# Transposing the first element's attended rows: TensorE into PSUM, or VectorE in 32x32 blocks and DRAM

## The chip, the cores and the metric

The kernel runs on one core of a Trainium2 chip. The metric is device time in microseconds (us) of one execution. The kernel before takes 826.79 us, the median of 3 runs (826.36 to 827.36).

A core has TensorE (PE: matmuls, with a separate weight load, PEld), VectorE (DVE), ScalarE (ACT), GpSimd (POOL) and SyncE (SP). Here SP issues nearly all DMA transfers. Each engine runs its own list of instructions in order and waits on semaphores of the others.

## The reference, cut to what matters

There are 4 elements of 512 tokens with 512 features. A cross-attention with 32 heads of 16 features is added to x, then an FFN is added.

```python
x = x + _L0_xattn_ref(_layernorm(x, axis=-1), ctx_1024, pos, pos, Wq, Wkv, Wout, bout)
x = x + _L0_ffn_ref(_layernorm(x, axis=-1), w_fc, w_proj)

# inside the FFN
h = bitlinear(x, w_fc)                    # layer norm, rounding that all but cancels, ternary weights
h = jax.nn.gelu(h, approximate=False)
return bitlinear(h, w_proj)
```

The FFN's first product is over the features. TensorE contracts over partitions, and x lies with tokens on the partitions. So the normalized rows after attention, called d here, must be turned: features on the partitions, tokens along the row. They are also split into a rounded high part and a low remainder[...].

## The kernel before, in words

**Attention.** The 4 elements have 8 groups of 4 heads each: 32 groups, counted from 0. A group works on 8 tiles (units) of each of three kinds, each tile 128 x 1024:

- Logits `lp` (`logits`, L526): TensorE multiplies queries and keys. VectorE takes the row maxima `mx` (`maxima`, L540).
- Scores `sp` (`exponentials`, L565 and L573): TensorE computes the transposed logits and subtracts the maxima by a second matmul. ScalarE takes the exponential `es` (L577).
- Products `av` (`weigh`, L587): TensorE multiplies exponentials and values, after each second unit.

The tiles `lp` and `sp` share one pool of three buffers, `ps_s`, each a pair of PSUM banks. A new tile takes one that an earlier tile has left: logits are left by VectorE, scores by ScalarE.

The order of the instructions on all five engines is written out by the program itself, which records them in the order in which Python calls them. A list of bursts holds three tiles each, scores and logits mixed. The logits run 12 to 15 units ahead of the scores. Between the bursts a planner puts small jobs (class `Chore`: projections, transposes) as a running credit allows. `put_off(k, f, 1)` defers a call to the end of burst k. The maxima of a whole group are turned by TensorE (`mtp`, L552), copied by ScalarE (`mrows`) and used by all its scores.

**The last element.** Groups 24 to 31 belong to the last element. During them, the first element's x is complete, and its FFN input is prepared, in four token tiles of 128 rows:

- `stats` (L730): VectorE computes mean and variance (`st`, `mv`), GpSimd the inverse deviation `r_a`. It is called in group 29, units 0 to 3.
- `prepare` (L739): VectorE writes the normalized rows `d`. It is called in group 30, units 0, 2, 4 and 6.
- `first_chore` and `first_T` (L780, L797): TensorE transposes the four 128x128 blocks of `d` into the PSUM buffer `tp_d` (L788). VectorE casts it to the high part `dTh` (L792) and subtracts for the low part `dTl` (L793). The jobs stand at the end of the planner's queue and run in group 31.

After the last group, the first matmuls of the FFN (`first`, `hp`, L1083) read `dTh` and `dTl` of element 0.

**The other elements** take another way, inside the FFN of the element before: `prepare`, then `turn` (L746: VectorE transposes in 32x32 blocks, `turned`), then `place` (L753: four DMAs lay the blocks in DRAM so that the whole is transposed), then `fetch_T` (L762: one DMA brings the tile back into `dTl`), then `split_T` (L772: ScalarE casts to `dTh`, VectorE subtracts in place).

SP also carries the stores and loads of the attended rows (`av_d`, `den`, `rden_d`, `rb`) and the loads of the FFN's second weights (`wproj`, two after each of the last four groups).

The functions that the change touches:

Of the kernel before, what the change touches and what calls it, by code (L numbers as in the profile page):

```python
# [9 lines left out]
F32 = mybir.dt.float32  # L10
F32R = mybir.dt.float32r
AF = mybir.ActivationFunctionType
ALU = mybir.AluOpType
# [18 lines left out]
def xattn_ffn(  # L32
# [264 lines left out]
    def put_off(k, f, end=0):  # L297
        later[end].setdefault(k, []).append(f)
# [440 lines left out]
    def prepare(i, pool, tag, bufs=2):  # L739
        d = pool.tile([P, D], F32, name=f"d{i}", tag=tag, bufs=bufs)  # L740
        nc.vector.tensor_scalar(
            d, x_sb[:, i, :], mv1[i][:, 0:1], f1[i], ALU.subtract, ALU.mult
        )
        return d

    def turn(i, d, pool, tag, bufs):  # L746

        b, t = divmod(i, NT)
        turned = pool.tile([P, D // HP, HP], F32, name=f"turned{i}", tag=tag, bufs=bufs)
        nc.vector.transpose(turned.rearrange("p n j -> p (n j)"), d)  # L750
        return turned

    def place(i, turned):  # L753
        b, t = divmod(i, NT)
        to = turned_d[b].rearrange("(n i) s -> i n s", i=HP)
        for a in range(P // HP):
            nc.sync.dma_start(
                to[:, :, t * P + a * HP : t * P + (a + 1) * HP],
                turned[a * HP : (a + 1) * HP],
            )  # L760
# [8 lines left out]
            turned_d[b].rearrange("(k p) s -> p k s", p=P)[:, :, cols],  # L769
        )  # L770

    def split_T(i):  # L772
        b, t = divmod(i, NT)
        if t == 0:
            dT[b][0] = big.tile([P, KD, S], F32R, name=f"dTh{b}", tag="aT", bufs=2)
        high, low = (x[:, :, t * P : (t + 1) * P] for x in dT[b])
        nc.scalar.copy(high, low.bitcast(F32))
        nc.vector.tensor_tensor(low, low.bitcast(F32), high.bitcast(F32), ALU.subtract)

    def first_T(i, d, tp, e):  # L780
        b, t = divmod(i, NT)
        if t == 0:
            dT[b] = (
                big.tile([P, KD, S], F32R, name=f"dTh{b}", tag="aT", bufs=2),
                big.tile([P, KD, S], F32R, name=f"dTl{b}", tag=f"va{b % 2}"),
            )
        for k in range(KD):
            nc.tensor.transpose(tp[:, k, :], d[:, k * P : (k + 1) * P], ident)  # L788

        def split():  # L790
            high, low = (x[:, :, t * P : (t + 1) * P] for x in dT[b])
            e(high, tp)  # L792
            nc.vector.tensor_tensor(low, tp, high.bitcast(F32), ALU.subtract)  # L793

        return split

    def first_chore(t, ready):  # L797
        split = []

        def step(p, _):  # L800
            tp = p.rearrange("p (k n) -> p k n", k=KD)
            split.append(first_T(t, first_d.pop(t), tp, nc.vector.tensor_copy))

        return Chore(f"tp_d{t}", 1, step, lambda p, k: put_off(k + 1, split[0]), 0.7, ready)


    n_groups = B * NG
# [96 lines left out]
    def when(i, u=0):  # L904
        return burst_of["s", i * NU + u]
# [17 lines left out]
    queue += a + projections(1) + c2 + c3  # L923
    n_prep = len(queue)
    queue += projections(2)
    queue += [first_chore(t, when(n_groups - 2, 2 * t + 1) + 1) for t in range(NT)]
    n_queue = len(queue)
    loads_behind = {
        f"kpk{b}_3": lambda b=b: (load_ctx(b + 1), load_trig(b + 1)) for b in range(B - 1)
# [7 lines left out]
    wanted = []  # L937
    urgent = []
    due = []
    av, es, first_d = {}, {}, {}  # L940
    open_chore = None
    credit = 0.0

    for k, burst in enumerate(bursts):
        run(k)
        for kind, s in burst:
            i, u = divmod(s, NU)
            if kind == "l":
                lp = logits(i, u)
                maxima(i, u, lp)  # L950
                if u == NU - 1:
                    urgent.append((k + 1, place_maxima(i)))
                continue
            b, g = divmod(i, NG)

            if u == 6 and 4 <= i + 3 < n_groups:
                wanted.append(i + 3)
            while wanted and {(wanted[0] // NG, wanted[0] % NG // 2, w) for w in "kq"} <= stored:
                load_stacks(wanted.pop(0))
            if (i, u) in loads_at:  # L960
                loads_at[i, u]()
            if u % 2 == 0 and (b == 0 and g == 0 or b < 2 and g == 5):
                norm1(b + 1 + (g > 0), u // 2)
            if u % 2 == 0 and u // 2 < XH and (b == 0 and g == 1 or b < 2 and g == 7):
                normed(b + 1 + (g > 1), u // 2)
            if g == 5 and u % 2 == 0:
                add_bias(b, u // 2)
            if u in (2, 6):
                c = 2 * i + u // 4
                if c < 2 * NW:  # L970
                    sum_chunk(c, k)
                c -= 18
                if 0 <= c < 2 * NW:
                    sign_chunk(c, k)
            if u == 6 and i in (8, 16):
                urgent.append((k, mean_abs(i // 8 - 1, (gam_fc, gam_pr)[i // 8 - 1])))
            if b == B - 1:
                if g >= NG - NS and u == NU - 1:
                    load_second(i)
                if g == 4 and u == 0:  # L980


                    wfc_sb = []
                    for n, tag in enumerate(("w0", "w1", "w4", "w5")):
                        wfc_sb.append(big.tile([P, F], F32R, name=f"wfc{n}", tag=tag))
                        nc.sync.dma_start(wfc_sb[n].bitcast(F32), wfc_d[n * P : (n + 1) * P, :])
                if g == 5 and u < NT:
                    stats(u)
                if g == 6 and u % 2 == 0:
                    first_d[u // 2] = prepare(u // 2, apool, "xh", XH)  # L990
            es[u] = exponentials(i, u)
            if u % 2:
                due.append((k + 1, i, u // 2, (es[u - 1], es[u])))
        run(k, 1)

        while due and due[0][0] <= k:
            _, j, c, e = due.pop(0)
            if c == 0:
                av[j] = ps_v.tile([P, S], F32, name=f"av{j}", tag="v")
            weigh(j, c, e, av[j])  # L1000
            if c == NT - 1:
                put_off(k + 1, lambda j=j, k=k: attended(j, av.pop(j), k + 1))

        credit = min(credit + (RATE if n_queue - len(queue) < n_prep else RATE_END), 3.0)
        used_bank = False
        next_urgent = urgent[0][0] if urgent else 10**6

        g_next = min(
            (burst_of["l", j * NU + NU - 1] + 1
             for j in range(n_groups)  # L1010
             if ("l", j * NU + NU - 1) in burst_of and burst_of["l", j * NU + NU - 1] + 1 >= k),
            default=10**6,
        )
        next_urgent = min(next_urgent, g_next)
        while True:
            if open_chore is None:
                if urgent and urgent[0][0] <= k:
                    if used_bank:
                        break
                    open_chore = urgent.pop(0)[1]  # L1020
                    open_chore.urgent = True
                elif queue and queue[0].ready <= k and not used_bank and credit >= queue[0].cost:
                    c = queue[0]
                    if next_urgent <= k or c.steps > 2.2 * (next_urgent - k):
                        break
                    open_chore = queue.pop(0)
                    open_chore.urgent = False
                else:
                    break
            left = open_chore.steps - open_chore.done  # L1030
            must = open_chore.urgent or next_urgent - k <= 1
            if not must and credit < open_chore.cost:
                break
            credit -= open_chore.cost
            if open_chore.go():
                if open_chore.name in loads_behind:
                    put_off(k + 1, loads_behind[open_chore.name], 1)
                open_chore.post(open_chore.p, k)
                open_chore = None
                used_bank = True  # L1040
# [138 lines left out]
    with tc.manual_schedule(engines=ordered):  # L1179
# [14 lines left out]
        for n in range(len(steps) + 4):  # L1194
# [21 lines left out]
            if on and b + 1 < B:  # L1216
                at = (10, 11, 12, 13) if b == 0 else (8, 10, 12, 13)
                for t in range(NT):
                    i = (b + 1) * NT + t
                    if f == at[t] - 6:  # L1220
                        stats(i)
                    elif f == at[t] - 4:
                        d = prepare(i, fpool, "d", 1)
                        place(i, turn(i, d, fpool, "turned", 1))
                        fetch_T(i)
                    elif f == at[t]:
                        split_T(i)
            if n == 3:
                nc.vector.tensor_copy(ones_r, ones)
            if n == 7:  # L1230
# [86 lines left out]
```

## Time and profile before

| What | us |
| --- | --- |
| Median of the runs | 826.79 |
| Profiled execution, its own time | 826.86 |
| Its span | 825.1 |
| PE busy | 803.9 |
| DVE busy | 609.7 |
| ACT busy | 472.3 |
| POOL busy | 300.2 |
| Transposes of d on TensorE (L788), start of the first and last | 551.5, 562.7 |
| Statistics of element 0 (L733), first to last start | 524.3, 533.6 |
| First FFN matmul (L1083) | 564.1 |
| Block transposes (L750), 12, mean | 0.712 |

A line of the profile names the source line, engine, operation, and the output and input tiles (`out<-in`). "Idle before" with an arrow names what ended an idle time. The chain is followed back from the last instruction of the execution, at each step to what released it. Times in a timeline count from the start of the span.

### The profile page before, as it was taken

What the parts mean: (1) busy time and instruction counts of PE and PEld (TensorE: products, weight loads), DVE (VectorE), ACT (ScalarE), POOL (GpSimd) and SP (SyncE); (2) the same over time, 40 slices, a digit from 0 to 9 for tenths busy, and PEclk for the clock granted to TensorE, in tenths of its full rate; (3) what the DMA queues carried; (4) which work ended last, traced back from release to release, by engine and by line L of the source; (5) the groups of instructions that cost most, each with busy time, mean ns of one, the idle gap of its engine ahead of it and who ended that gap; (6) DMA issues with size and microseconds to landing.
All of it is one profiled execution on the core that took longest, in us unless ns stands there. A gap on an engine that the chain in (4) does not pass through costs nothing.

```text
span 825.1 us, 14410 instructions
## 1 busy us (share of the span) xinstructions
PE 803.9 (97%) x5524; PEld 424.0 (51%) x5524; DVE 609.7 (74%) x846; ACT 472.3 (57%) x664; POOL 300.2 (36%) x299
## 2 busy tenths in 40 slices
PE   9999999999999999999999999999999999999996
PEld 5234443344343334433343334336668888888884
DVE  7798677787868888778767876855746885875755
ACT  3257667676675556656555665576335455555542
POOL 2546275563933656576515731210200210211001
PEclk9999999999999999999999999999999999999999
DMA  7768596578785477968644677443130140240101
GB/s 252 217 211 299 189 317 220 176 245 282 238 288 194 169 283 232 314 197 274 215 154 165 224 228 276 149 140 105 40 63 14 40 101 14 68 87 0 52 1 51
DMA packets 107604, 139.94 MB, mean 170 GB/s; under 512 B 37776, under 2 KB 45456, under 8 KB 107024
## 3 DMA queue, kind: packets, MB, share of 16 engines
q1 hardware_dynamic: 106608, 138.38, 51.2%
q8 instruction: 43, 0.70, 0.4%
q10 hardware_dynamic: 928, 0.66, 0.3%
q14 instruction: 25, 0.20, 0.1%
HBM read 80.87 MB, written 57.08 MB: 167 GB/s over the span
## 4 chain that ended last, share of the span: by engine, by line
PE 79%; DVE 11%; DMA 4%; issue 2%; ACT 1%; POOL 1%; SPq 1%; ACTq 0%; DVEq 0%; POOLq 0%
PE hp L1083 14%; PE fp L1121 14%; PE av L587 12%; PE sp L565 7%; PE lp L526 7%; DVE mx L540 6%; PE sp L573 5%; PE op L346 4%; PE qpq L346 4%; PE kpk L346 3%; PE vp L346 3%; PE op L1207 2%; DMA q_st<-q_d 2%; PE mtp L552 2%; DVE ws L684 1%
## 5 line engine op out<-in xcount | busy, mean ns | idle before, releaser
L540 DVE TENSOR_REDUCE mx<-lp 128x2 f32<-128x1024 f32 x256 | 305.1, 1216 | 98.6 <-PE lp L526 98.3
L577 ACT ACTIVATE es<-sp 128x1024 f32<-128x1024 f32 x256 | 254.5, 1025 | 138.7 <-PE sp L573 129.0
L587 PE MATMUL av<-es,va 128*32 128x512 f32 x1024 | 136.2, 604 | 0.0
L565 PE MATMUL sp<-q_st,k_st 64*128 64x512 f32 x512 | 114.5, 443 | 6.3 <-DVE mx L540 5.5
L526 PE MATMUL lp<-k_st,q_st 64*128 64x512 f32 x512 | 112.3, 435 | 3.9 <-DMA q_st<-sl_q 1.9
L1091 ACT ACTIVATE h<-hp,gam_fc 128x512 f32<-128x512 f32 x64 | 44.1, 689 | 116.8 <-PE hp L1083 114.5
L573 PE MATMUL sp<-mrows,sel 64*128 64x512 f32 x512 | 101.4, 392 | 0.2 <-ACT mrows L556 0.2
L1121 PE MATMUL fp<-wproj,hh 128*128 128x512 f32 x256 | 101.0, 394 | 0.0
L1083 PE MATMUL hp<-dTh,wfc 128*128 128x512 f32 x256 | 100.2, 392 | 0.0
L1083 PE MATMUL hp<-dTl,wfc 128*128 128x512 f32 x256 | 99.8, 390 | 0.0
L1121 PE MATMUL fp<-wproj,hl 128*128 128x512 f32 x256 | 99.7, 389 | 0.0
L565 PEld LDWEIGHTS sp<-q_st,k_st 64*128 64x128 f32 x512 | 48.0, 184 | 79.4 <-DVE mx L540 37.9
L526 PEld LDWEIGHTS lp<-k_st,q_st 64*128 64x128 f32 x512 | 48.2, 185 | 75.4 <-ACT es L577 41.9
L1110 DVE TENSOR_TENSOR acc<-acc,h 128x512 f32<-128x512 f32 x56 | 39.5, 706 | 54.8 <-ACT h L1091 54.8
L626 POOL TENSOR_TENSOR aT<-aT,rb 128x512 f32<-128x512 f32 x16 | 21.3, 1333 | 130.1 <-DMA rb<-rden_d 126.9
L346 PE MATMUL qpq<-xT,wq_sb 128*32 128x512 f32 x512 | 62.9, 594 | 0.7 <-ACT xT L383 0.7
L1157 POOL TENSOR_TENSOR m<-m 128x4 f32<-128x4 f32 x4 | 0.8, 201 | 158.6 <-DVE m L1156 158.6
L1083 PEld LDWEIGHTS hp<-dTh,wfc 128*128 128x128 f32 x256 | 48.0, 188 | 11.6 <-DVE dTh L792 0.8
L1121 PEld LDWEIGHTS fp<-wproj,hh 128*128 128x128 f32 x256 | 48.1, 188 | 10.8 <-issue 0.9
L1121 PEld LDWEIGHTS fp<-wproj,hl 128*128 128x128 f32 x256 | 48.1, 188 | 10.7 <-issue 0.7
L1083 PEld LDWEIGHTS hp<-dTl,wfc 128*128 128x128 f32 x256 | 48.1, 188 | 10.0
L573 PEld LDWEIGHTS sp<-mrows,sel 64*128 64x128 f32 x512 | 48.3, 185 | 6.0 <-ACT mrows L556 0.8
(154 smaller groups left out, 1054.8 us busy)
## 6 DMA issues: line engine op xcount, KB each, us to landing
k_st<-k_d SPq DMA_DIRECT2D x31, 512.0 KB
q_st<-q_d SPq DMA_DIRECT2D x31, 512.0 KB
av_d<-avs SPq DMA_DIRECT2D x32, 256.0 KB
k_d<-sh_k SPq DMA_DIRECT2D x30, 256.0 KB
k_d<-sl_k SPq DMA_DIRECT2D x30, 256.0 KB
q_d<-sh_q SPq DMA_DIRECT2D x30, 256.0 KB
q_d<-sl_q SPq DMA_DIRECT2D x30, 256.0 KB
wm<-in_wfcT SPq DMA_DIRECT2D x16, 256.0 KB
```

What stands on the lines that cost most here:

```text
L346: nc.tensor.matmul(p[j * HP : (j + 1) * HP, :], w[:, j * HP : (j + 1) * HP], x, start=start, stop=stop,)
L526: nc.tensor.matmul(lp[:, h, :], q_st[i][rows, r, t * P : (t + 1) * P], k_st[i][rows, r, :], start=True, stop=True,)
L540: nc.vector.tensor_reduce(mx[i][:, t, :, r], lp, AX.X, ALU.max, negate=True)
L565: nc.tensor.matmul(sp[:, h, :], k_st[i][rows, r, c * P : (c + 1) * P], q_st[i][rows, r, :], start=True, stop=False,)
L573: nc.tensor.matmul(sp[:, h, :], sel[rows, r, :], mrows[i][rows, :], start=False, stop=True)
L577: nc.scalar.activation(es, sp, AF.Exp, scale=1.0 / math.sqrt(HD))
L587: nc.tensor.matmul(av[j * HP : (j + 1) * HP, :], va[b % 2][:, c, v0 : v0 + HP], es[r][:, h, :], start=c == 0, stop=c == NT - 1,)
L626: nc.gpsimd.tensor_tensor(aT[b][:, n, :], aT[b][:, n, :], rb, ALU.mult)
L1083: nc.tensor.matmul(hp, wfc_sb[k][:, f * P : (f + 1) * P], dT[b][half][:, k, :], start=half == 0 and k == 0, stop=half == 1 and k == KD - 1,)
L1091: nc.scalar.activation(hid[b, f], hp, AF.Gelu, scale=gam_fc[:, 0:1])
L1110: nc.vector.tensor_tensor(acc[b][0], old, x, ALU.add)
L1121: nc.tensor.matmul(outs[b][t], parts[b, f][half][:, t * P : (t + 1) * P], wproj_sb[f], start=half == 0 and f == 0, stop=half == 1 and f == ...
```

## The change

Element 0 now takes the way of the other elements, inside the attention of the last element:

- The statistics are called in group 28, units 0 to 3, one group earlier.
- In group 29, units 0, 2, 4 and 6, `prepare` is followed at once by `turn`. Both tiles come from the pool tag `xh` with three buffers.
- `place` is deferred by one burst, `fetch_T` by four.
- In group 31, units 0, 2, 4 and 6, GpSimd casts the high part; one burst later VectorE subtracts for the low part.
- The four planner jobs with 16 TensorE transposes are gone, and with them the casts and subtractions that read PSUM.
- `split_T` is divided into `high_T` and `low_T`. The other elements use ScalarE for the first as before.

```diff
+    def high_T(i, e):
         b, t = divmod(i, NT)
         if t == 0:
             dT[b][0] = big.tile([P, KD, S], F32R, name=f"dTh{b}", tag="aT", bufs=2)
-        high, low = (x[:, :, t * P : (t + 1) * P] for x in dT[b])
-        nc.scalar.copy(high, low.bitcast(F32))
+        high, low = parts_T(i)
+        e(high, low.bitcast(F32))
+
+    def low_T(i):
+        high, low = parts_T(i)
         nc.vector.tensor_tensor(low, low.bitcast(F32), high.bitcast(F32), ALU.subtract)
...
-    queue += [first_chore(t, when(n_groups - 2, 2 * t + 1) + 1) for t in range(NT)]
...
-                if g == 5 and u < NT:
+                if g == 4 and u < NT:
                     stats(u)
-                if g == 6 and u % 2 == 0:
-                    first_d[u // 2] = prepare(u // 2, apool, "xh", XH)
+                if g == 5 and u % 2 == 0:
+                    t = u // 2
+                    d = turn(t, prepare(t, apool, "xh", XH), apool, "xh", XH)
+                    put_off(k + 1, lambda t=t, d=d: place(t, d), 1)
+                    put_off(k + 4, lambda t=t: fetch_T(t), 1)
+                if g == 7 and u % 2 == 0:
+                    put_off(k, lambda t=u // 2: high_T(t, nc.gpsimd.tensor_copy), 1)
+                    put_off(k + 1, lambda t=u // 2: low_T(t), 1)
...
-                        split_T(i)
+                        high_T(i, nc.scalar.copy)
+                        low_T(i)
```

More of the change, by code (lines that the diff above doesn't have):

```diff
@@ L770, in fetch_T, with parts_T @@
         )
-    def split_T(i):
+    def parts_T(i):
+        b, t = divmod(i, NT)
+        return (x[:, :, t * P : (t + 1) * P] for x in dT[b])
+    def high_T(i, e):
         b, t = divmod(i, NT)
@@ L775, in split_T @@
             dT[b][0] = big.tile([P, KD, S], F32R, name=f"dTh{b}", tag="aT", bufs=2)
-        high, low = (x[:, :, t * P : (t + 1) * P] for x in dT[b])
-        nc.scalar.copy(high, low.bitcast(F32))
+        high, low = parts_T(i)
+        e(high, low.bitcast(F32))
+    def low_T(i):
+        high, low = parts_T(i)
         nc.vector.tensor_tensor(low, low.bitcast(F32), high.bitcast(F32), ALU.subtract)
[L780 to L804, printed above, removed]
     n_groups = B * NG
@@ L939, in xattn_ffn @@
     due = []
-    av, es, first_d = {}, {}, {}
+    av, es = {}, {}
     open_chore = None
```

## The prediction

> **What bounds the kernel now.** I read the page first: the busy line and the chain's shares.
>
> ```profile
> PE 803.9 (97%) x5524; PEld 424.0 (51%) x5524; DVE 609.7 (74%) x846; ACT 472.3 (57%) x664; POOL 300.2 (36%) x299
> ...
> PE 79%; DVE 11%; DMA 4%; issue 2%; ACT 1%; POOL 1%; SPq 1%; ACTq 0%; DVEq 0%; POOLq 0%
> ```
>
> TensorE carries most of the chain, but that is an average over 825 us. The change touches the last attention groups alone (28 to 31, counted from 0), so next come the busy times by stretch: start:end, length, busy us of PE, PEld, DVE, ACT and POOL, granted clock, DMA share, GB/s.
>
> ```profile
> 500.00:520.00 20.00, 20.00 (x158) 8.15 (x156) 14.77 (x17) 11.23 (x13) 2.52 (x2) 1.00 0.74 290
> 520.00:530.00 10.00, 9.34 (x76) 3.50 (x76) 7.97 (x10) 5.74 (x7) 2.31 (x5) 1.00 0.80 265
> 530.00:540.00 10.00, 9.58 (x68) 3.64 (x67) 8.95 (x14) 5.49 (x6) 4.99 (x8) 1.00 0.14 35
> 540.00:550.00 10.00, 9.45 (x66) 3.82 (x66) 5.21 (x8) 7.00 (x8) 0.72 (x1) 1.00 0.40 133
> ```
>
> From 500 to 520 TensorE has no gap. From 520 to 540 it has gaps, and VectorE is 80 to 90% busy. After 540 VectorE falls idle. The chain in order of time (start, length, what) shows the limits:
>
> ```profile
> 523.18 1.23 DVE mx L540
> 524.41 0.61 DVE st L733
> ...
> 527.47 0.61 DVE st L733
> ...
> 530.94 0.62 DVE st L733
> ...
> 533.68 0.61 DVE st L733
> ...
> 540.12 1.23 DVE mx L540
> 541.35 0.45 DVE d L741
> 541.80 1.14 DVE mx L540
> ```
>
> So VectorE sets the pace from 523 to 535.6, with all four statistics (st) on the path, and again at 540 to 543. Then TensorE and ScalarE alternate until 564.2, where the FFN starts; of the four transposes of the first element (tp_d), only the last two (560.09 and 562.37, 0.59 each) are on the chain. The first two lie under exponentials.
>
> Last, the timeline at 540 shows how logits (lp) and scores (sp) hand three pairs of PSUM banks round:
>
> ```profile
> 539.91 0.39 PE L565 MATMUL sp<-q_st,k_st 64*128 64x512 f32 x2
> 540.38 0.39 PE L526 MATMUL lp<-k_st,q_st 64*128 64x512 f32 x2
> 540.65 1.03 ACT L577 ACTIVATE es<-sp 128x1024 f32<-128x1024 f32 x1 [0.80 <-PE sp L573]
> 541.70 0.50 PE L565 MATMUL sp<-q_st,k_st 64*128 64x512 f32 x2
> 542.54 1.03 ACT L577 ACTIVATE es<-sp 128x1024 f32<-128x1024 f32 x1
> 542.99 0.50 PE L565 MATMUL sp<-q_st,k_st 64*128 64x512 f32 x2 [0.32 <-DVE mx L540]
> ```
>
> The scores at 539.91 are read by the exponential from 540.65 to 541.68, yet the next logits start at 540.38, because they have another pair.
>
> **The change, part by part.**
>
> *Transposes out.* Sixteen matmuls at 0.146 us (four in 0.585) are 2.3 us of TensorE. The first two groups of four hide under exponentials and give nothing. The last four exponentials run without a gap from 559.32 to 563.09, whatever the transposes do; the last products need the last of them. Without the fourth group they end about 0.4 us earlier. The first FFN matmul follows at once, but the third FFN tile waits for the first GELU (568.07), and that waits behind the table load and the last store, which hang on the last exponential. Gain between 0 and 1.2 (both chain entries); I take 0.3.
>
> *Rule against row.* The Trainium skill, "VectorE: DVE Perf Modes", Rules for kernel authors, says to transpose 128x128 on TensorE if PSUM is an acceptable target, since VectorE turns only 32x32 blocks. It speaks against the change. The rows: per tile, before, TensorE 0.585 and VectorE 0.69 (L792) + 0.69 (L793) = 1.38; after, VectorE 0.71 (L750) + 0.68 (the row of L778) = 1.39, GpSimd 0.63 to 0.69 (the casts of L421), and five DMAs. By the rule alone the change loses; by the rows VectorE's total is equal and TensorE gains 2.3. What decides is where the 0.71 lands: before, both VectorE passes ran after 552, where it idled; now the block transposes run in its full stretch.
>
> *VectorE, 508 to 541.* The built order has the four statistics in group 28: after the 4th to 7th logits tiles of group 29 (508 to 516). They are behind one another there, so up to 0.9 us may show as waits, but the stretch from 523 is relieved of 4 x 0.82 = 3.3 us (524.32 to 525.14 is one step). Into it come four pairs of normalizing and turning, after the 4th and 8th tile of group 30 and the 2nd and 4th of group 31: 4 x (0.45 + 0.71 + 0.05) = 4.8. Net +1.5 by the maxima at 538 and 540. The trace has 0.23 and 0.81 of VectorE idle before these two, but TensorE delivers later too, since it waits for the banks those maxima free. Bounds 0.5 (both gaps filled) and 1.6; I take +1.2, nearer the upper, as the chain is on VectorE on both sides. All four transposes before this point are queued ahead of maxima, and score tiles wait for these.
>
> *PSUM banks.* The built programs differ in something that the diff doesn't say. Before, the pairs of scores 30/0, logits 31/6, scores 30/1, logits 31/7, scores 30/2 start at banks 4, 2, 0, 4, 2: always another. After, they start at 4, 4, 0, 2, 0. So logits 31/6 must wait for the exponential of scores 30/0, with nothing of TensorE's between, and scores 30/2 for that of scores 30/1. Priced by the timeline: the exponential of the tile at 539.91 ends at 541.68, its successor could start at 541.75 instead of 540.38: +1.37. The products and scores 30/1 behind it move too, to 543.07; their exponential starts 0.84 later (541.70 to 542.54) and ends at 544.94; scores 30/2 start at 545.0 instead of 542.99 + 1.37 = 544.36: +0.64. Sum 2.0. Bounds: 0, if the lateness of VectorE covers it wholly, and 2.0. It isn't covered, as the waits are for ScalarE and come after scores that are late already; I take 2.0. Here the Trainium skill has a rule: "Perfetto Trace Analysis", Optimizing Tensor Performance, lets independent matmul groups rotate through different banks, so that one is emptied while the next is filled. Where the rotation is kept, as in before, the sum is +0.9; with the row's price for the broken one it is +2.9.
>
> *Late again afterwards?* The transposed maxima of group 31 go to TensorE at 546.55, and their copies end at 544.5: 2 us of cover. From there scores, exponentials and products follow in one cycle, so a delay at 544 reaches 564 whole.
>
> *DMAs.* Sixteen small stores and four fetches enter SP's queue, and none leaves. A store's issue takes 0.49, four take 2; the fetch behind the FFN's first four was issued 1.6 us after the last one (601.07 against 599.48). Store 1 stands behind the reciprocals' store and its spreading load (533.16, 534.65), so it is issued at 535.3 to 537.3 and lands near 538.9. The fourth turn needs its buffer and runs at about 540: it just fits. The third needs store 0, landed near 530. Behind it in SP stand the av store (542.45) and two loads of second weights, which wait for TensorE (548.33) as before and aren't pushed back; the fourth fetch comes after these and goes out near 552 to 553. With the megabyte ahead of it (at 250 GB/s, 4 us) it lands by 556; cast and subtraction end near 558, 9 us before an FFN that starts at 567. Cost 0, and up to 2 if store 1 is late. GpSimd's casts come ahead of only the product at 571.16.
>
> *Sum.* 1.2 + 2.0 - 0.3 = +2.9 on the profiled execution of 826.86 (span 825.1, 1.76 around it): 829.8. That execution lies 0.07 above the median of the runs, so 829.7.
>
> **Rivals.**
> 1. *Only VectorE's shift counts* (1.2 - 0.3): 827.7. For it: logits 31/6 are no use before VectorE is free. Against: its maxima waited only 0.9 (540.85 to 541.71) and the products behind it in order wait with it.
> 2. *A wait for the stores takes over*: if store 1 lands 2 us later, VectorE stands at the turn with all maxima behind it: 831 to 833. GpSimd and VectorE also slow each other here: the addition at 571.68 took 1.79 instead of about 0.7 beside a product of GpSimd of 1.76; the third and fourth pairs run beside such work at 538 to 541, and half as much again on four pairs is +2.4. For: the margin is 1 us. Against: DMA share is 0.14 there.
> 3. *Faster*: the gaps of ScalarE behind 546 (0.95, 1.64, 0.96 and 1.40) soak up all lateness, and the 2.3 us of transposes is won: 824.5. It decides once the cycle there absorbs more than 3.2. Against: these gaps end with products that come after scores in TensorE's order.
> 4. *It doesn't do what it says*: the operands come too late. They would have to be 9 us late.
>
> **How the numbers follow.** The main case (829.7, own range 828.6 to 831.0) has 0.66, rival 1 0.14, rival 2 with 4 0.13, rival 3 0.07. About 0.2% (1.65 us) is what a measurement can tell from no change. Slower is the main case, rival 2, and a little of rival 1: 0.81; same is most of rival 1: 0.13; faster 0.06. The range takes half of rival 1 and most of rival 2: 827.9 to 831.9.
>
> **What would show it.** Right: a logits tile of group 31 that waits for es where it waited for nothing, and a scores tile after it; turned among the maxima on the chain; no st on it; first hp about 2.5 us later; no wait of hp for dTh or dTl. Wrong: the last exponential of group 31 at its old time (the bank step or VectorE's fails), a DVE wait for turned_d (rival 2), or hp waiting for POOL (rival 4).

## The result, and the profile after

The changed kernel takes 831.94 us (median; 830.28 to 833.67), the kernel before, in the same comparison, 827.58 (826.36 to 828.70). The ratio is 1.0055, with a 95% interval of 1.0041 to 1.0068: about 4.5 us slower. The forecast was slower by 2.9, at 829.7, with a range up to 831.9. The direction is right; the time lies 2.2 above the forecast and just outside the range. Of these 2.2, 0.8 belong to the kernel before, which measured 826.79 when the forecast was made and 827.58 here; the rest comes of a change of 4.4 to 4.5 where 2.9 was forecast.

The profiled execution took 830.54 (span 828.7). The page of the changed kernel, busy line and chain:

```profile
PE 802.6 (97%) x5508; PEld 422.5 (51%) x5508; DVE 609.0 (73%) x846; ACT 472.1 (57%) x664; POOL 302.4 (36%) x303
...
PE 82%; DVE 11%; ACT 2%; DMA 2%; issue 2%; POOL 1%; SPq 0%; ACTq 0%; DVEq 0%; POOLq 0%
```

VectorE's total is what it was (609.7 before) and TensorE has 16 instructions less. Of the engines in this line GpSimd alone has more work: 302.4 against 300.2, with the four casts, and it is busy for 36% of the span. Yet the kernel is slower: the loss must be in the order of things. The busy times of the changed kernel by stretch (columns as before):

```profile
500.00:520.00 20.00, 18.79 (x150) 7.37 (x142) 17.36 (x24) 10.38 (x13) 7.98 (x12) 1.00 0.78 292
520.00:530.00 10.00, 9.41 (x70) 3.61 (x72) 8.01 (x9) 5.08 (x6) 0.00 (x0) 1.00 0.93 281
530.00:540.00 10.00, 8.70 (x62) 3.42 (x58) 9.79 (x15) 5.59 (x6) 0.22 (x1) 1.00 0.28 58
540.00:550.00 10.00, 7.61 (x58) 2.97 (x54) 6.62 (x9) 5.59 (x6) 3.48 (x4) 1.00 0.99 236
```

TensorE loses about 1.2 us of work in the first stretch (20.00 before), 0.9 from 530 to 540 and 1.8 from 540 to 550. GpSimd has moved: 2.52 us before and 7.98 after in the first stretch. At 530 VectorE is full (9.79). The granted clock is 1.00 in all four.

The chain of the changed kernel in order of time says what TensorE waited for:

```profile
514.21 0.61 DVE st L733
...
516.17 1.07 DVE mparts L544
...
517.27 1.20 DVE mparts L545
...
526.15 0.71 DVE turned L750
...
542.27 1.03 ACT es L577
...
543.35 0.50 PE lp L526 x2
...
546.69 0.50 PE sp L565 x2
```

The statistics (st) are on the chain in their new place, the block transposes (turned) too, and the matmuls at 543.35 and 546.69 follow an exponential each. New and not forecast are the two `mparts` entries: the cast and the subtraction that split the maxima of group 29 for their turn by TensorE. In the kernel before they took 0.18 each there:

```profile
516.63 0.18 DVE L544 CAST mparts<-mx 128x16 fp32r<-128x16 f32 x1
516.84 0.18 DVE L545 TENSOR_TENSOR mparts<-mx,mparts 128x16 fp32r<-128x16 f32 x1
```

**How the runs below are compared.** Executions differ by a microsecond or so before the change has acted. So beside the medians I use a stretch within the profiled execution: from the start of the first exponential of group 24 (L577) to the start of the FFN's first GELU (`h`, L1091 before, L1077 after). Before it takes 121.86 us (445.48 to 567.34), after 126.28 (444.65 to 570.93): +4.42, all of the measured difference of about 4.5. It grows in two places. At the first exponential of group 30 it is +2.45, two exponentials later +4.52, and 0.10 is won back at the end.

### The profile page after: what moved, and what is told of

Its sections match the earlier page's. It is cut to its first block, busy times and chain, and to the rows that moved or that the text cites. A ratio compares the mean times of both kernels' runs of the same rounds, so it can differ in the third digit from the quotient of the medians.

```text
span 828.7 us, 14412 instructions
## 1 busy us (share of the span) xinstructions
PE 802.6 (97%) x5508; PEld 422.5 (51%) x5508; DVE 609.0 (73%) x846; ACT 472.1 (57%) x664; POOL 302.4 (36%) x303
## 4 chain that ended last, share of the span: by engine, by line
PE 82%; DVE 11%; ACT 2%; DMA 2%; issue 2%; POOL 1%; SPq 0%; ACTq 0%; DVEq 0%; POOLq 0%
PE hp L1069 14%; PE fp L1107 14%; PE av L587 12%; PE sp L565 8%; PE lp L526 7%; DVE mx L540 6%; PE sp L573 5%; PE qpq L346 5%; PE op L346 4%; PE vp L346 3%; PE kpk L346 3%; PE op L1193 2%; PE mtp L552 2%; ACT es L577 1%; DMA q_st<-q_d 1%
## 5 line engine op out<-in xcount | busy, mean ns | idle before, releaser
L577 ACT ACTIVATE es<-sp 128x1024 f32<-128x1024 f32 x256 | 254.5, 1025 | 139.8 <-PE sp L573 130.2
L1077 ACT ACTIVATE h<-hp,gam_fc 128x512 f32<-128x512 f32 x64 | 44.1, 689 | 116.8 <-PE hp L1069 114.6
```

The source lines that it names most:

```text
L577: nc.scalar.activation(es, sp, AF.Exp, scale=1.0 / math.sqrt(HD))
L1077: nc.scalar.activation(hid[b, f], hp, AF.Gelu, scale=gam_fc[:, 0:1])
```

## What holds VectorE: GpSimd's bias additions

GpSimd adds the output bias to the last element's rows, four times 128x512 (L339). Its timeline before, with `r_a` (L226, L227) standing for the inverse deviations that wait for the statistics:

```profile
505.03 1.28 POOL L339 TENSOR_TENSOR x_sb<-x_sb,bout_sb 128x512 f32<-128x512 f32 x1
525.32 0.19 POOL L226 TENSOR_SCALAR r_a<-mv 128x1 f32<-128x1 f32 x1 [19.01 <-DVE mv L734]
...
529.17 1.27 POOL L339 TENSOR_TENSOR x_sb<-x_sb,bout_sb 128x512 f32<-128x512 f32 x1
...
535.37 1.28 POOL L339 TENSOR_TENSOR x_sb<-x_sb,bout_sb 128x512 f32<-128x512 f32 x1
```

And after:

```profile
515.39 0.55 POOL L227 TENSOR_TENSOR r_a<-r_a,mhalf 128x1 f32<-128x1 f32 x1
515.91 3.74 POOL L339 TENSOR_TENSOR x_sb<-x_sb,bout_sb 128x512 f32<-128x512 f32 x3
539.78 1.29 POOL L626 TENSOR_TENSOR aT<-aT,rb 128x512 f32<-128x512 f32 x1 [20.12 <-DMA rb<-rden_d]
```

Before, the additions stood between the deviations in GpSimd's list and were held apart by their waits. After, the four deviations come first, and three additions run back to back, 515.91 to 519.65. VectorE's timeline of the changed kernel shows what meets them:

```profile
516.17 1.06 DVE L544 CAST mparts<-mx 128x16 fp32r<-128x16 f32 x1
517.27 1.20 DVE L545 TENSOR_TENSOR mparts<-mx,mparts 128x16 fp32r<-128x16 f32 x1
```

The cast ends at 517.23 and the subtraction at 518.47, about where the first addition (to 517.2) and the second (to 518.4) end: each seems to stand until GpSimd's instruction is through. The kernel before had this too, elsewhere. Its rows of the tile `mparts` (min/median/max ns, first and last start):

```profile
L544 DVE CAST mparts<-mx x32: 175/178/1278, 40.0 to 544.1; 128x16 fp32r<-128x16 f32 x32
L545 DVE TENSOR_TENSOR mparts<-mx,mparts x32: 175/178/1256, 40.2 to 544.3; 128x16 fp32r<-128x16 f32 x32
```

The maximum is seven times the median. In that profile the pair at 267.88 and 269.09 takes 1.18 and 1.22 beside two of these additions. Of the 19 instances longer than 0.3, each overlaps an instruction of GpSimd on 128x512, and 17 end within 0.05 us of the end of one. The prediction read neither row.

## Experiments

### The order of the score buffers alone, in the changed kernel

My theory at this point: the additions cost 1.9, the order in which scores and logits get their three buffers 2.0. This kernel gives each tile of the pool the buffer that it has in the kernel before. `BANKS` is a string with one digit for each tile.

```diff
+    def s_tile(name):
+        n = len(taken)
+        taken.append(name)
+        return ps_s.tile([P, 2, S], F32, name=name, tag=f"s{BANKS[n]}", bufs=1)
...
-        lp = ps_s.tile([P, 2, S], F32, name=f"lp{i}_{u}", tag="s")
+        lp = s_tile(f"lp{i}_{u}")
```

> The changed kernel, but logits and scores take the three PSUM buffers in the very order of the kernel before (a table of tags); nothing else differs. Theory A (the change costs three things in groups 28 to 31: banks that don't rotate, about 2.0 us; GpSimd's bias additions holding VectorE's two small casts of the maxima, about 1.9; the block transposes, the rest): the last exponential of group 31 comes 2.0 us earlier than in the changed kernel, logits 31/6 and scores 30/2 wait for no exponential, and the time is about 2.5 us over the kernel before. Theory B (VectorE's load alone; banks cost nothing): no change, 4.5 us over before.

830.99, ratio 1.0045 (1.0027 to 1.0063). The stretch is +3.94: a gain of 0.48, not 2.0. The wait for the buffers is gone, but at the first exponential of group 30 the delay is now 4.40 instead of 2.45. Something else had lain behind the buffers; the third run (both edits) shows what.

### The additions alone, in the changed kernel

```diff
-            if g == 5 and u % 2 == 0:
+            if g == (5 if b < B - 1 else 6) and u % 2 == 0:
                 add_bias(b, u // 2)
```

The last element's additions are called in group 30 instead of 29.

> The changed kernel, but the last element's four bias additions on GpSimd are called in group 30 instead of 29, so that they come behind the product at 540 in GpSimd's order. Theory A: the two casts of group 29's maxima (1.06 and 1.20 us in the changed kernel) fall back to 0.18 each, and the time falls by 1.3 to 1.9 us, to about 3 over before. Theory B (the casts' length is hidden): no change of the time, or under 0.3.

829.26, ratio 1.0026 (1.0014 to 1.0037). The stretch is +2.56: a gain of 1.86. VectorE's timeline of this kernel:

```profile
516.55 0.18 DVE L544 CAST mparts<-mx 128x16 fp32r<-128x16 f32 x1
516.76 0.18 DVE L545 TENSOR_TENSOR mparts<-mx,mparts 128x16 fp32r<-128x16 f32 x1
```

The same instructions at the same place, without an addition beside them, take 0.18 again. They had taken 1.90 more, and 1.86 is won: the cause is shown, and VectorE passes it on whole.

### Both

The two edits together.

> Both edits of the two runs before this one together: banks in the order of the kernel before, bias additions in group 30. Theory A: what is left is the block transposes and the moved statistics less the TensorE transposes: about 1.3 us over before. Theory B: 4.5 over before. If the two overlap, the sum of the gains is under 3.3 us.

829.66, ratio 1.0031 (1.0020 to 1.0041). The stretch is +1.96, 0.6 better than with the additions alone; the medians (829.66 and 829.26) can't tell the two apart. VectorE's timeline has the rest (this kernel's lines stand 16 lower: L766 is the L750 of the changed kernel):

```profile
541.20 0.71 DVE L766 STREAM_TRANSPOSE turned<-d 128x512 f32<-128x512 f32 x1 [1.49 <-DMA turned_d<-turned]
```

The fourth block transpose waits for a buffer whose store to DRAM hasn't landed. The changed kernel has the same wait:

```profile
541.21 0.71 DVE L750 STREAM_TRANSPOSE turned<-d 128x512 f32<-128x512 f32 x1 [1.28 <-DMA turned_d<-turned]
```

There the logits behind it wait for their buffer anyway. With the buffers in the old order, the store wait comes to the front.

### The order of the buffers alone, in the kernel before

Here everything is the kernel before, but its tiles get the buffers in the changed kernel's order.

```diff
-        sp = ps_s.tile([P, 2, S], F32, name=f"sp{i}_{u}", tag="s")
+        sp = s_tile(f"sp{i}_{u}")
```

> The kernel before, but with the order of PSUM buffers of the changed kernel; all instructions stay. Theory A: 2 to 3 us slower than before (3 if nothing else is late there to cover a part of it). Theory B: no difference.

830.59, ratio 1.0036 (1.0024 to 1.0048). The stretch is +2.63. TensorE's and ScalarE's timeline of this kernel (L542 are logits, L581 scores, L593 exponentials):

```profile
541.08 1.02 ACT L593 ACTIVATE es<-sp 128x1024 f32<-128x1024 f32 x1 [0.89 <-PE sp L589]
542.16 0.49 PE L542 MATMUL lp<-k_st,q_st 64*128 64x512 f32 x2 [1.18 <-ACT es L593]
...
544.41 1.02 ACT L593 ACTIVATE es<-sp 128x1024 f32<-128x1024 f32 x1
545.48 0.50 PE L581 MATMUL sp<-q_st,k_st 64*128 64x512 f32 x2 [0.95 <-ACT es L593]
```

In the kernel before, the logits at this place waited for nothing. In the changed kernel:

```profile
542.27 1.02 ACT L577 ACTIVATE es<-sp 128x1024 f32<-128x1024 f32 x1 [0.88 <-PE sp L573]
543.35 0.50 PE L526 MATMUL lp<-k_st,q_st 64*128 64x512 f32 x2 [1.17 <-ACT es L577]
...
545.61 1.02 ACT L577 ACTIVATE es<-sp 128x1024 f32<-128x1024 f32 x1
546.69 0.50 PE L565 MATMUL sp<-q_st,k_st 64*128 64x512 f32 x2 [0.95 <-ACT es L577]
```

The same two waits, 1.18 and 0.95 here, 1.17 and 0.95 there. From the first to the third exponential of group 30 the delay grows by 2.06, in the changed kernel by 2.07; the other 0.5 of this run comes before, late in group 29. A change that moves no instruction but only hands out the same three buffers in another order costs 2.6 us.

### Both, with four buffers for the turned rows

```diff
-                    d = turn(t, prepare(t, apool, "xh", XH), apool, "xh", XH)
+                    d = turn(t, prepare(t, apool, "xh", XH), apool, ("rot", "oth")[t % 2], 2)
```

> The third experiment (additions out of the way, scores' and logits' buffers in the old order) left about 2.0 us at the start of the feed-forward part, with the fourth block transpose still waiting 1.5 us for the first store. Here the transposed rows rotate over four buffers instead of two, so that no transpose waits for a store. Theory (the rest is that wait and VectorE's own extra time): the wait disappears from the fourth transpose, and the feed-forward part starts about 0.8 to 1.3 us later than in the kernel before, its time about 828.3 to 828.7. Rival (the rest has nothing to do with the store: transposes and row reads by themselves): no gain against the third experiment, 829.5 or so.

828.02, ratio 1.0008 (0.9998 to 1.0019): no slower than before by this measurement. The stretch is +0.54, 1.42 less than with the three buffers that `d` and the turned rows share, where the wait had been 1.49. The fourth transpose starts 0.02 after its `d`:

```profile
540.32 0.71 DVE L766 STREAM_TRANSPOSE turned<-d 128x512 f32<-128x512 f32 x1
```

With the additions away, the buffers in order and the store wait gone, nearly all of the loss is accounted for: 4.42 = 1.86 (additions) + 2.02 (buffers, with the store behind them) + 0.54. The split holds for this order of repairs: the buffers repaired first win 0.48 alone.

### The changed kernel with the store wait alone removed

The same line as above, with buffers of scores and logits as the changed kernel has them, and the additions where it has them.

> The changed kernel, its buffers of scores and logits in the order that it has, with four buffers for the transposed rows. Theory (in the changed kernel the store wait lies behind the wait for a scores buffer): the fourth transpose no longer waits, but the time stays within 0.4 us of the changed kernel's, at about 831.5 to 832. Rival (the store wait is on the path): 1.2 us or more are gained, 830.7 or less.

832.64, ratio 1.0056 (1.0037 to 1.0074), where the changed kernel had 1.0055. The wait costs nothing there, as expected. The profiled execution reads +6.06 in the stretch, but has a mishap of its own. The busy times by stretch of this execution, around it:

```profile
524.00:527.00 3.00, 3.00 (x16) 1.01 (x20) 1.08 (x1) 1.74 (x2) 0.00 (x0) 0.52 1.03 298
```

The clock granted to TensorE was 0.52 for 3 us, and in the exponentials at that place 1.6 us appear at once (+2.08 in the changed kernel, +3.70 here). Without them it is about +4.5, which agrees with the medians.

### No block transposes

Both repairs and four buffers, but the rows of element 0 are stored without being turned.

```diff
-                    d = turn(t, prepare(t, apool, "xh", XH), apool, ("rot", "oth")[t % 2], 2)
+                    d = prepare(t, apool, ("rot", "oth")[t % 2], 2).rearrange("p (n j) -> p n j", j=HP)
```

> As the kernel with four buffers and both repairs, but the four block transposes of element 0's attended rows are left out: the rows go to DRAM as they are, so the feed-forward part of element 0 works on rows that were not transposed (that part of the result is left out). It measures what the transposes themselves cost there: 4 instructions of about 0.7 us. Theory (VectorE's queue carries them to the exponentials at their full length): about 2.5 to 3.5 us less than with them, so some 825 to 826 us, faster than before. Rival (VectorE has slack in that stretch and the transposes lie in it): under 1 us less.

825.71, ratio 0.9975 (0.9963 to 0.9987). The stretch is -1.77, so the four transposes cost 2.31 there, of their 4 x 0.71 = 2.84. They do stand in VectorE's full stretch and pass on four fifths of their length, somewhat less than expected. The +0.54 that was left is thus the sum of a cost of 2.31 for turning and a gain of 1.77 from all else in this kernel.

### The two moves without the transposes

The kernel before, TensorE transposing, with the statistics in group 28 and the last element's additions in group 30.

```diff
-            if g == 5 and u % 2 == 0:
+            if g == (5 if b < B - 1 else 6) and u % 2 == 0:
                 add_bias(b, u // 2)
...
-                if g == 5 and u < NT:
+                if g == 4 and u < NT:
                     stats(u)
```

> The kernel before, with TensorE's transposes kept, and only two of its placements changed: the row statistics of element 0 one group earlier, as the change has them, and the last element's bias additions one group later, out of the casts' way. Theory (casts held by GpSimd were costing in the old place too, and early statistics are harmless once the additions are gone): 0.5 to 1.6 us faster than before, 825.7 to 826.8. Rival (moving the statistics is itself what costs): 0.5 us or more slower than before.

826.97, ratio 0.9995 (0.9984 to 1.0006). The stretch is -0.86; the medians can't tell it from none. At the first exponential of group 30 it is -1.96; 1.1 is lost right behind, where the additions now stand. VectorE's normalization of the first tile meets them:

```profile
540.19 1.61 DVE L741 TENSOR_SCALAR d<-x_sb,mv,r_a 128x512 f32<-128x512 f32 x1
```

It takes 0.54 in the kernel before; here GpSimd's four additions run from 538.98 to 544.16. The same collision, moved.

### The statistics' move alone

```diff
-                if g == 5 and u < NT:
+                if g == 4 and u < NT:
                     stats(u)
```

> The kernel before with one thing changed: element 0's row statistics one group earlier, as the change places them. Transposes stay with TensorE, the additions keep their rule. Theory (early statistics let GpSimd's queue run its three bias additions just when VectorE casts the maxima of the next group): the casts take about 1.1 and 1.2 us instead of 0.18 each, and with the 0.8 us that the same kernel gained with the additions moved, the start of the feed-forward part comes about 1.1 us later than before (0.5 to 1.9), the time about 828.7. Rival (the stretched casts belong to the block transposes or to GpSimd's roundings): the casts keep 0.18 us and the kernel is as fast as before or faster by up to 1 us.

827.91, ratio 0.9998 (0.9990 to 1.0007). VectorE's timeline:

```profile
516.41 1.06 DVE L544 CAST mparts<-mx 128x16 fp32r<-128x16 f32 x1
517.51 1.20 DVE L545 TENSOR_TENSOR mparts<-mx,mparts 128x16 fp32r<-128x16 f32 x1
```

There is no block transpose and no rounding on GpSimd in this kernel, and the long casts are there to the hundredth: they come from moving the statistics, through the order of GpSimd's list. My expectation of the sum was wrong, though. The delay is +2.06 at the first exponential of group 29, and by group 30 it is -0.05, because the group that lost the statistics gives back as much. The stretch is -0.03. The early statistics are worth about 1.9 at group 30 (-1.96 with the additions away), and the casts spend it.

### The statistics in group 25, TensorE transposing

The additions in group 30 as above, `stats` in group 25 (`g == 1`).

```diff
-                if g == 5 and u < NT:
+                if g == 1 and u < NT:
                     stats(u)
```

> The kernel before with the statistics of element 0 three groups earlier than the change has them, and the last element's bias additions one group later, so that neither falls among the last maxima. TensorE keeps its transposes. Theory (the statistics cost where VectorE has no slack, and the additions where the casts are): 0.8 us or more gained, so 825 to 826.5 us, under both kernels. Rival (VectorE is as full there, and what is gained at the end is paid earlier): within 0.4 us of the kernel before.

826.47, ratio 0.9985 (0.9976 to 0.9993): a little faster than both kernels, with the transposes left on TensorE. The stretch is -0.55; of the -1.57 at group 30, the additions again take 1.0.

### The change's way, off the last maxima

Statistics in group 25, transposes in group 28, four buffers, the last element's additions in group 30.

```diff
-                if g == 4 and u < NT:
+                if g == 1 and u < NT:
                     stats(u)
-                if g == 5 and u % 2 == 0:
+                if g == 4 and u % 2 == 0:
                     t = u // 2
-                    d = turn(t, prepare(t, apool, "xh", XH), apool, "xh", XH)
+                    d = turn(t, prepare(t, apool, "xh", XH), apool, ("rot", "oth")[t % 2], 2)
```

> The change's way (VectorE transposes, placed through DRAM, GpSimd rounds) with everything moved off the last maxima: statistics three groups earlier, the transposes one group earlier, four buffers for the turned rows, the last element's additions one group later; the buffers of scores and logits fall as the allocator has them. Theory (the cost was of place, not of kind): 0.5 to 2 us faster than before, 825 to 826.5. Rival (four transposes of 0.7 us cost 2.3 us wherever they stand, as in the kernels with and without them): 0.5 us slower than before or more.

827.36, ratio 0.9995 (0.9985 to 1.0004), the stretch -0.65. So the change's way need not be slower than before. By the medians it is no gain either: between the theory and its rival.

The run does not show that turning is free in group 28. Several things moved at once, and the order of the buffers changed with them: here no logits wait for an exponential from 538 to 551, and no scores tile waits for one longer than 0.36, so this kernel doesn't pay the 2.0 of the changed one. At the first exponential of group 30 the delay is -0.21, where the run before, with the same statistics and the additions moved likewise, has -1.57. The difference of 1.36 is what turning and normalizing in group 28 cost up to there, if the order of the buffers adds nothing. The two end alike because that kernel then loses 1.0 to the additions.

### The same, with the transposes in group 26

```diff
-                if g == 4 and u % 2 == 0:
+                if g == 2 and u % 2 == 0:
```

This line is against the run just told of.

> As the kernel with the transposes one group earlier, but with them three groups earlier, directly behind the statistics. Theory (cost of place): as that kernel within 0.5 us, or a little better, 825 to 826.5. Rival (the transposes cost the same wherever they stand): 0.5 us slower than before or more.

832.29, ratio 1.0042 (1.0023 to 1.0061), the stretch +4.84. The theory failed. The time lies where the rival had it (0.5 slower or more), but only a part is the rival's: about 2 us come in group 26, where VectorE now normalizes and turns the rows; the run without turning gave 2.31 for the turning alone. About 4 come in group 29, of which 1.6 is won back by the third exponential of group 30. TensorE's timeline there:

```profile
534.84 0.50 PE L526 MATMUL lp<-k_st,q_st 64*128 64x512 f32 x2 [3.14 <-DMA q_st<-q_d]
```

The queries of group 31 came late. SP's timeline of this kernel shows them go out late:

```profile
495.01 4.82 SPq L757 DMA_DIRECT2D turned_d<-turned  x4
...
509.37 2.14 SPq L966 DMA_DIRECT2D wfc<-wfc_d  x4
513.57 0.32 SPq L605 DMA_DIRECT2D av_d<-avs  x1
526.59 0.60 SPq L616 DMA_DIRECT2D den<-av_d  x1
...
528.38 0.46 SPq L512 DMA_DIRECT2D q_st<-q_d  x1
```

In the changed kernel the four weight loads (4 MB, L966) went out at 500.80, the read of `den` at 517.78 and the queries at 519.56. Here SP was busy with stores and fetches of turned rows to 508, the 4 MB left at 509.37, and SP stood 13 us for the store at 513.57 before it read `den` and then loaded the queries. That the 4 MB held up that store is my reading; it wasn't tried. Single executions of this kernel reach from 827.11 to 833.93, further apart than those of any other here, and one alone was profiled.

## Why the prediction was right or wrong

- **VectorE, +1.2 (0.5 to 1.6): the step that failed, by a term left out.** At the first exponential of group 30 the changed kernel is 2.45 late. With the additions away it is 0.56 late (0.97 with the buffers in the old order too), within the bounds; the additions make the other 1.9. The sum counted VectorE's instructions at their undisturbed length and moved the statistics without GpSimd's list behind them. Its sign "no st on it" failed too: the statistics are on the chain, at 514.21. Rival 2 named the mutual slowing, but put it beside the third and fourth pairs at 538 to 541; there the normalization took 0.53 and the transpose 0.71, undisturbed. It struck 23 us earlier, on instructions that the change doesn't touch.
- **Within that term:** "relieved of 3.3" was worth about 1.9 at group 30 (the statistics' move with the additions away), and of the 4.8 for the four pairs the 2.84 of turning cost 2.31. Both are less than their length, so the net came out near the lower bound.
- **PSUM banks, +2.0: right.** From the first to the third exponential of group 30 the delay grows by 2.07 (2.45 to 4.52), with the two waits where they were foretold. In the kernel before, the order alone costs 2.63, 2.06 of it at these two waits.
- **TensorE's transposes, -0.3:** 0.10 measured from the third exponential of group 30 to the GELU (4.52 to 4.42). They were hidden almost wholly. The measured sum is then 2.45 + 2.07 - 0.10 = 4.42, against 1.2 + 2.0 - 0.3 = 2.9.
- **DMAs, cost 0: right in sum, wrong in its reason.** Store 1 was to be issued until 537.3 and to land at 538.9. Its last issue ended at 538.63, and the transpose that waited for it started at 541.21: 2.6 behind it, not 1.6. It didn't "just fit"; it was 1.28 late and lay behind the wait for the buffers. With the buffers in order it cost 1.4. The rest held: the last subtraction came at 559.18, 8.6 us before the first FFN matmul (567.82), which waits for neither part.
- **The rule against the row:** by the Trainium skill, "VectorE: DVE Perf Modes", Rules for kernel authors, which sends a 128x128 transpose to TensorE if PSUM is an acceptable target, the change was to lose; by the rows, VectorE's total was to stay and the place to decide. The change did lose, but the rule's reason isn't what the runs show: VectorE's total stayed (609.0 against 609.7), and additions and buffers, with the store behind them, made 3.9 of the 4.42. The same block transposes one group earlier, with four buffers, the statistics and additions moved and another order of the buffers, leave a kernel as fast as before (0.9995). With statistics and additions moved likewise and the transposes on TensorE it is 0.9985. That median is 0.9 lower, but the intervals overlap and the stretches are alike (-0.55 and -0.65), so no run here settles which engine is the better. Turning was not free on VectorE in any of the three places tried: 2.31 in group 29 and, with the normalizing, about 1.4 in group 28 and 2 in group 26.
- **The rivals:** the time is that of rival 2 (831 to 833), in part by luck. Its wait for the store was there but hidden, and its mutual slowing came from another pair of instructions. Rival 1 fails by the two waits for the buffers. Rival 3 fails as well: the delay of 4.52 at the third exponential of group 30 is still 4.51 at the last of group 31. Rival 4 fails because no operand came late.

## What to carry to other kernels

When a change moves an instruction that another engine waits for, write out that engine's list as well: what stood apart because of the wait may now run in one piece. Look at the maximum of a row beside its median; a short instruction with a maximum seven times its median is one that something else can hold. And where a pool hands out buffers, compare the buffer of each tile in the two built programs: an order costs 2.6 us here by itself, and a removed wait may only show the next one.

## What the runs showed of the hardware

VectorE's cast and subtraction on 128x16 tiles in SBUF stood until GpSimd's 128x512 addition was through: 1.06 and 1.20 us for 0.18, in the changed kernel and with the statistics' move alone, and 0.18 with the addition elsewhere. A 128x512 normalization took 1.61 for 0.54. A maximum, which reads PSUM, kept its 1.23 us at 539.05 beside additions from 538.98 on (the kernel with the two moves and no block transposes). In the changed kernel the block transpose at 541.21 took its 0.71 beside an addition at 541.03, and an addition of VectorE's that reads one operand from PSUM (L648, 518.39) took 0.68, its usual time, beside GpSimd's at 518.40. So not every instruction is held, and which are was not tried out further.
